# A rational layer in a four-layer convolution kernel: where the powers of its input are computed, and when

## The chip, the cores and the metric

The kernel runs on one core of a Trainium2 chip. Five engines work side by side, each through its own queue in order: TensorE (PE; PEld is its weight load), VectorE (DVE), ScalarE (ACT), GpSimd (POOL) and SyncE (SP), which only sends transfers. ACT can send transfers too. They meet at semaphores. The metric is the device time of one execution in microseconds (us); the kernel before took 11252.07 us, the median of three runs (11250.59 to 11255.03).

## The reference, cut to what matters

Four residual layers work on `x` of shape (8, 16, 128, 128) in float32. The change concerns the third, `x = x + _L2_conv_ref(_gn(x), A, Bc)`, a convolution whose weights are rational functions:

```python
def _gn(v, G=8, eps=1e-5):
    g = v.reshape(B_, G, C_ // G, H_, W_)
    ...
    return ((g - m) / jnp.sqrt(s + eps)).reshape(v.shape)

def _L2_conv_ref(x, A, Bc):          # K = 3, DEG_P = 6, DEG_Q = 4
    ...
    xp = jnp.pad(x, ((0, 0), (0, 0), (pad, pad), (pad, pad)))
    wins = jnp.stack([xp[:, :, i:i + H, j:j + W] for i in range(K) for j in range(K)])
    pw = wins[..., None] ** jnp.arange(DEG_P, dtype=x.dtype)
    P = jnp.einsum('pbchwi,fcpi->fpbchw', pw, A)
    Q = 1.0 + jnp.abs(jnp.einsum('pbchwi,fcpi->fpbchw', pw[..., 1:1 + DEG_Q], Bc))
    out = jnp.sum(P / Q, axis=(1, 3))
```

So each normalised value is needed to the powers 1 to 5; for each of the nine places of the window, each input channel and each of 16 filters there is one quotient P/Q, and the quotients are summed over places and channels.

## The kernel before

The residual `x` lies in SBUF (on-chip memory) as 128 partitions, one for each image and channel, by 128 x 128 pixels. The layers run one after the other. The rational layer has three parts.

*Powers.* `group_stats` (line 918) gives each partition its mean and `rs`, the inverse deviation. `powers(r0)`, line 929, makes the five powers of two image rows: two POOL memsets for the left and right border, the first power on DVE (L934), second and fourth as squares on ACT (L942, L944), third and fifth as products on POOL (L943, L945), each in a tile of its own with one buffer. Five transfers (L947) write them to `yd2` in DRAM, whose padded image has 130 x 130 pixels. Its top and bottom border rows are written once, from a tile of zeros (`zt`, L927).

*Turns.* `turn(r0, g)`, line 955, loads ten rows of powers of half of the images (even or odd, g) into four of the eight tiles `f`, 16 transfers on SP (L959). A row of ones in `f` stands for the power zero.

*Couples.* The work of the layer is a list of 1152 couples: 16 blocks of eight rows, two halves g of the images, two parts k of four rows, nine window places n, and two i. A block has 72 couples. For each couple PE forms the denominators `pd` and the numerators `pn` in PSUM (L971). With d the denominator, ACT takes t = |d| (two `absolute`, L992), u = ln(1 + t) (`ln`) and u = exp(-u) (`exp`, both recorded by the helper at L152), an approximate 1/(1 + t). DVE then corrects it by one Newton step: `step`, t = (1 + t)u (L1003); `times`, u = pn u (two, L1009); `ratio`, u = (t - 2)u for half of the tile (L1016). `correction` has POOL form the product v = t u of the other half (L1024). PE sums over the channels (`over_channels`, L1055), and when a group of four rows is finished DVE adds it to `x` (L1067) and takes its statistics (L1068).

The order of this loop, lines 1087 to 1119, is written by hand: the products of couple m + 1 are made beside those of couple m, and a helper `in_turn(engine, ins)` ties each ACT and DVE instruction of the couples to the one before it by an order. Within these ties a scheduler places each engine's instructions and adds the waits. The instructions of `powers` have no such tie: L1079 to L1083 call it for the first 16 rows, then the loop calls it four times in the first couple of a block, for the rows of the block after next:

```python
if (c.k, c.n, c.i) == (0, 0, 0):
    if c.g == 0 and c.r0 + 16 < H:
        for r in range(c.r0 + 16, c.r0 + 24, 2):
            powers(r)
    if c.r0 + 8 * c.g < H:
        turn(c.r0 + 8 * c.g, 1 - c.g)
c.ln()
```

Buffers: the tiles t and u have four each, v three, `pn` two, `pd` one, each power one.

Of the kernel before, what the change touches and what calls it, by code (L numbers as in the profile page):

```python
# [9 lines left out]
F32 = mybir.dt.float32  # L10
AF = mybir.ActivationFunctionType
ALU = mybir.AluOpType
# [4 lines left out]
B, C, H, W = 8, 16, 128, 128  # L17
BC = B * C
HW = H * W
HP, WP = H + 2, W + 2  # L20
# [80 lines left out]
def kernel(  # L101
# [20 lines left out]
    nc = tc.nc  # L122
# [6 lines left out]
    dram = ctx.enter_context(tc.tile_pool(name="scratch", bufs=1, space=DRAM))  # L129
# [5 lines left out]
    def k_(name):  # L135
        n, lo, hi = _WHERE[name]
        return const[:n, lo - from_ : hi - from_]
# [3 lines left out]
    sets = {AF.Exp: "exp_ln", AF.Ln: "exp_ln", AF.Tanh: "sigmoid", AF.Sigmoid: "sigmoid"}  # L141
# [36 lines left out]
    def group_stats(bn, tag):  # L178

        mv = stat.tile([BC, 2], F32, name="mv")  # L180
        nc.vector.bn_aggr(mv, bn.rearrange("p a b -> p (a b)"))
        with tc.tile_pool(name="ps_stat" + tag, bufs=1, space=PSUM) as ps:
            pm = ps.tile([BC, 1], F32, name="pm")
            mm(pm, k_("pair"), mv[:, 0:1], start=True, stop=True)
            mean = stat.tile([BC, 1], F32, name="mean")
            nc.vector.tensor_copy(mean, pm)
            dm = stat.tile([BC, 1], F32, name="dm")
            nc.vector.tensor_sub(dm, mv[:, 0:1], mean)
            e2 = stat.tile([BC, 1], F32, name="e2")
            nc.vector.scalar_tensor_tensor(e2, dm, dm, mv[:, 1:2], op0=ALU.mult, op1=ALU.add)  # L190
            pv = ps.tile([BC, 1], F32, name="pv")
            mm(pv, k_("pair"), e2, start=True, stop=True)
            var = stat.tile([BC, 1], F32, name="var")
            nc.vector.tensor_scalar_add(var, pv, EPS)

        s0 = stat.tile([BC, 1], F32, name="s0")
        lut(s0, var, AF.Sqrt)
        s1 = stat.tile([BC, 1], F32, name="s1")
        nc.vector.reciprocal(s1, s0)
        nc.vector.scalar_tensor_tensor(s1, s1, var, s0, op0=ALU.mult, op1=ALU.add)  # L200
        nc.vector.tensor_scalar_mul(s1, s1, 0.5)
        rs = stat.tile([BC, 1], F32, name="rs")
        nc.vector.reciprocal(rs, s1)
        d = stat.tile([BC, 1], F32, name="d")
        nc.vector.scalar_tensor_tensor(d, mean, -1.0, rs, op0=ALU.mult, op1=ALU.mult)
        return mean, dm, rs, d
# [3 lines left out]
    def in_turn(engine, ins):  # L210

        if engine in chain:
            tc.add_manual_dep(ins, chain[engine].name, order, reason="in turn")
        chain[engine] = ins
        return ins
# [3 lines left out]
    for n in range(5):  # L219
        t = cpool.tile([BC, BC], F32, name=f"w1_{n}")  # L220
        nc.gpsimd.memset(t, 0.0)
        for b in range(B):
            r = slice(b * C, (b + 1) * C)
# [10 lines left out]
    with ExitStack() as l0:  # L234
        wp = l0.enter_context(tc.tile_pool(name="w0", bufs=1))
        with tc.tile_pool(name="x0", bufs=2) as xp:
# [6 lines left out]
            mean0, _, rs0, d0 = group_stats(bn0, "0")  # L243
# [25 lines left out]
        for a in range(2):  # L269
            src = aff_d[:, a : a + 1].rearrange("(d p g c) a -> p g c (d a)", p=2, g=2, c=C)  # L270
            for odd in range(2):
                for g in range(2):
                    for i in range(3):
                        r = 64 * (g ^ odd) + 16 * i
# [6 lines left out]
        for i in range(3):  # L281
            for g in range(2):
                r = slice(64 * g + i * 16, 64 * g + i * 16 + 16)
# [44 lines left out]
        act = l0.enter_context(tc.tile_pool(name="act0", bufs=1))  # L328
        tmp = l0.enter_context(tc.tile_pool(name="tmp0", bufs=1))
# [326 lines left out]
        for n in range(-2, NCH + 3):  # L656
# [62 lines left out]
            if any((new, old, ahead)):  # L719
                r = var.finish()  # L720
# [42 lines left out]
    bn2 = cpool.tile([BC, NCH, 6], F32, name="bn2")  # L763
    with ExitStack() as l1:
        wp = l1.enter_context(tc.tile_pool(name="w1", bufs=1))
        tmp = l1.enter_context(tc.tile_pool(name="tmp1", bufs=3))
# [8 lines left out]
        for t, src, least in ((wa, a2, 0), (wb, q2, 1)):  # L775
            for s in range(2):
                dense = wp.tile([128, 144], F32, name="dense", bufs=2)
                nc.gpsimd.memset(dense, 0.0)
                for u in range(4):
                    for i in range(1, src.shape[0] // C + least):  # L780
                        lo, r = 32 * (u ^ s) + 4 * (i - 1), C * (i - least) + 4 * u
# [21 lines left out]
        w = wp.tile([128, 144, 9], F32, name="w")  # L803
# [11 lines left out]
        for s in range(4):  # L815
            for p in range(2):
                if 0 <= s - p < 3:
# [4 lines left out]
                    for g in range(2):  # L822
# [3 lines left out]
                            k_("image")[rows, 2 * s + g : 2 * s + g + 1],  # L826
                        )

        mean, dm, rs, _ = group_stats(bn1, "1")
        xmax = wp.tile([BC, 1], F32, name="xmax")  # L830
        nc.vector.tensor_reduce(xmax, top, AX.X, ALU.max)
# [82 lines left out]
    with ExitStack() as l2:  # L914
        wp = l2.enter_context(tc.tile_pool(name="w2", bufs=1))
        tmp = l2.enter_context(tc.tile_pool(name="tmp2", bufs=1))
        gather = k_("gather").rearrange("p (k g m) -> p k g m", k=2, g=2)
        mean, _, rs, _ = group_stats(bn2, "2")


        yd2 = dram.tile([4 * B, 20, HP, WP], F32, name="yd2")
        yv = yd2.rearrange("g (i c) h w -> g i c h w", i=5)
        zt = wp.tile([BC, WP], F32, name="zt")
        nc.gpsimd.memset(zt, 0.0)
        for i in range(5):
            for r in (0, HP - 1):
                nc.sync.dma_start(yv[:, i, :, r, :], zt)  # L927

        def powers(r0):

            y = [tmp.tile([BC, 2, WP], F32, name=f"y{i}") for i in range(1, 6)]
            nc.gpsimd.memset(y[0][:, :, 0:1], 0.0)
            nc.gpsimd.memset(y[0][:, :, WP - 1 : WP], 0.0)
            nc.vector.tensor_scalar(  # L934
                y[0][:, :, 1 : 1 + W],
                x[:, r0 * W : (r0 + 2) * W].rearrange("p (a b) -> p a b", a=2),
                mean,
                rs,
                ALU.subtract,
                ALU.mult,  # L940
            )
            nc.scalar.activation(y[1], y[0], AF.Square)  # L942
            nc.gpsimd.tensor_mul(y[2], y[1], y[0])  # L943
            nc.scalar.activation(y[3], y[1], AF.Square)  # L944
            nc.gpsimd.tensor_mul(y[4], y[3], y[0])  # L945
            for i in range(5):
                nc.sync.dma_start(yv[:, i, :, 1 + r0 : 3 + r0, :], y[i])  # L947

# [1 line left out]
        for t in fs:  # L952
            nc.gpsimd.memset(t, 1.0)

        def turn(r0, g):
            for q in range(NP):
                for u in range(4):
                    lo = 32 * (u ^ (q % 2))
                    nc.sync.dma_start(  # L959
                        fs[g * NP + q][lo : lo + 20],  # L960
                        yd2[4 * (2 * q + g) + u, :, r0 : r0 + 10, :],
                    )
# [67 lines left out]
        def products(num, ab, den):  # L1030


            todo = []
            if den:
                den.pd[1 - ab] = ps.tile([128, 2, 512], F32, name="pd")
                todo.append(product(den.pd[1 - ab], wb, *den.at(1 - ab)))
            if num:
                num.pn[ab] = ps.tile([128, 2, 512], F32, name="pn", bufs=2)
                todo.append(product(num.pn[ab], wa, *num.at(ab)))
            for _ in range(4):  # L1040
                for p in todo:
                    last["product"] = next(p)
# [33 lines left out]
            for i in range(NP // 2)  # L1076
        ]
        count = len(couples)
        for r in range(0, 10, 2):  # L1079
            powers(r)  # L1080
        turn(0, 0)
        for r in range(10, 16, 2):
            powers(r)  # L1083
        products(None, 1, couples[0])
        couples[0].absolute(0)
        products(None, 0, couples[0])
        for m in range(count + 4):
            c, before, then = (couples[i] if 0 <= i < count else None for i in (m, m - 1, m + 1))
            if c:
                c.absolute(1)  # L1090
            if c or before:
                products(before, 1, then)
            if m % 2 and m >= 3 and m - 3 < count:
                over_channels(couples[m - 3 : m - 1], 0)
            if m % 2 == 0 and m >= 4 and m - 4 < count:
                over_channels(couples[m - 4 : m - 2], 2)
            if before:
                before.times(1)
                before.ratio()
            if c:  # L1100
                if (c.k, c.n, c.i) == (0, 0, 0):
                    if c.g == 0 and c.r0 + 16 < H:
                        for r in range(c.r0 + 16, c.r0 + 24, 2):
                            powers(r)
                    if c.r0 + 8 * c.g < H:
                        turn(c.r0 + 8 * c.g, 1 - c.g)
                c.ln()
                if then:
                    then.absolute(0)
                products(c, 0, then)  # L1110
            if m % 2 and m >= 3 and m - 3 < count:
                over_channels(couples[m - 3 : m - 1], 1)
            if c:
                c.exp()
                c.step()
            if before:
                before.correction(c.stepped if c else before.stepped)
            if c:
                c.times(0)
# [6 lines left out]
    with ExitStack() as l3:  # L1126
        wp = l3.enter_context(tc.tile_pool(name="w3", bufs=1))
        tmp = l3.enter_context(tc.tile_pool(name="tmp3", bufs=2))
        mean, _, rs, d = group_stats(bn3, "3")
# [51 lines left out]
        c = curve(v, WP)  # L1181
# [284 lines left out]
```

## Time and profile before

| what | value |
|---|---|
| median of three runs | 11252.07 us |
| profiled execution | 11250.13 us, of which its span is 11248.3 us |
| granted PE clock, mean | 0.971 of full speed |
| PE busy | 8843.7 us (79%) |
| DVE busy | 9068.7 us (81%) |
| ACT busy | 8780.2 us (78%) |
| POOL busy | 4873.1 us (43%) |
| rational layer, first step to last step | 3584.05 to 10560.0 us of the span |
| POOL products for powers 3 and 5 | 64 x 1187 ns and 64 x 1140 ns |
| DVE first power | 64 x 427 ns |
| ACT squares | 64 x 417 ns and 64 x 410 ns |

The busy times of whole-span engines mix four layers with different limits, so a change in one layer is judged from that layer's stretch. In the lines below a group of instructions is named by its line, engine and operation, then out<-in by the tiles' names and shapes, the count, the busy time in us, the mean ns of one, and the idle time of the engine just before these instructions with the one that ended it.

### The profile page before, as it was taken

To read this page: it belongs to the slowest core of one execution; us is meant where nothing else is said; L and a number is where in the kernel's file an instruction comes from. 1 tells how busy PE (TensorE), PEld (TensorE's weight loads), DVE (VectorE), ACT (ScalarE), POOL (GpSimd) and SP (SyncE) were. 2 spreads that over 40 slices of the span, in tenths; PEclk is the share of its full clock that TensorE was granted. 3 is DMA by queue.
4 is the path that set the end of the run, shared out by engine and by line. 5 is a ranking of instruction groups with operands and counts; after the bars stand their busy time and mean duration, and the time that the engine had idled before them with its cause. 6 is when DMAs were issued, how large, how long until landed. Compare 5 with 4: busy or idle time off the path is not lost.

```text
span 11248.3 us, 173864 instructions
## 1 busy us (share of the span) xinstructions
PE 8843.7 (79%) x72372; PEld 2092.2 (19%) x72372; DVE 9068.7 (81%) x6829; ACT 8780.2 (78%) x7107; POOL 4873.1 (43%) x2681
## 2 busy tenths in 40 slices
PE   5999999999986777777777777777777777777788
PEld 1222222222222111111111111111111111111122
DVE  3555555555555799999999999999999999999865
ACT  2555555555545799999999999999999999999876
POOL 3555555555553633333334333334334333343300
PEclk8999999999998899999999999999999999999899
DMA  1000000000003300000000000000000000000022
GB/s 47 13 15 15 12 13 15 15 13 13 14 6 94 119 7 7 13 7 7 8 12 7 7 13 7 7 13 7 7 13 7 7 13 7 7 7 7 20 54 50
DMA packets 189391, 203.91 MB, mean 18 GB/s; under 512 B 46777, under 2 KB 155449, under 8 KB 186553
## 3 DMA queue, kind: packets, MB, share of 16 engines
q1 hardware_dynamic: 180264, 190.81, 6.4%
q8 instruction: 569, 9.32, 0.3%
q10 hardware_dynamic: 8336, 1.97, 0.1%
q14 instruction: 222, 1.81, 0.1%
HBM read 107.15 MB, written 60.04 MB: 15 GB/s over the span
## 4 chain that ended last, share of the span: by engine, by line
DVE 44%; PE 31%; ACT 14%; issue 5%; POOL 2%; DMA 1%; SPq 1%; DVEq 0%; ACTq 0%; POOLq 0%
DVE t L1003 22%; PE banks L360 17%; DVE u L1009 14%; PE pn L971 10%; ACT t L992 9%; DVE y L518 2%; PE acc L1322 2%; ACT u L152 1%; POOL y L527 1%; DVE x L538 1%; ACT hid L152 1%; PE pd L971 1%; DMA yd<-y 1%; DVE x L630 1%; SPq L1286 1%
## 5 line engine op out<-in xcount | busy, mean ns | idle before, releaser
L971 PE MATMUL pn<-f,wa 32*64 32x512 f32 x18432 | 3413.7, 625 | 1711.6 <-DVE u L1009 1687.3
L1024 POOL TENSOR_TENSOR v<-t,u 128x1024 f32<-128x1024 f32 x1152 | 2739.8, 2378 | 4017.4 <-DVE t L1003 3871.3
L1009 DVE TENSOR_TENSOR u<-pn,u 128x1024 f32<-128x1024 f32 x2304 | 2713.7, 1219 | 117.7
L971 PE MATMUL pd<-f,wb 32*64 32x512 f32 x18432 | 2601.0, 626 | 161.1 <-ACT t L992 94.6
L1003 DVE SCALAR_TENSOR_TENSOR t<-t,u 128x2048 f32<-128x2048 f32 x1152 | 2630.6, 2283 | 33.9 <-ACT u L152 33.6
L992 ACT ACTIVATE t<-pd 128x1024 f32<-128x1024 f32 x2304 | 2338.4, 1015 | 311.2 <-PE pn L971 304.7
L152 ACT ACTIVATE u<-t 128x2048 f32<-128x2048 f32 x1152 | 2202.5, 1912 | 51.9 <-PE acc L1055 15.9
L152 ACT ACTIVATE u<-u 128x2048 f32<-128x2048 f32 x1152 | 2190.7, 1902 | 0.0
L971 PEld LDWEIGHTS pn<-f,wa 32*64 32x64 f32 x18432 | 750.0, 131 | 3775.4 <-DVE u L1009 3246.1
L1016 DVE SCALAR_TENSOR_TENSOR u<-t,u 128x1024 f32<-128x1024 f32 x1152 | 1418.5, 1231 | 37.9
L152 ACT ACTIVATE hid<-banks 128x1024 f32<-128x1024 f32 x576 | 571.8, 1023 | 1049.6 <-PE banks L360 1047.7
L1055 PE MATMUL acc<-u,const 128*32 128x512 f32 x9216 | 1257.2, 618 | 1.8 <-DVE u L1016 1.8
L527 POOL TENSOR_TENSOR y<-y 128x1536 f32<-128x1536 f32 x256 | 895.0, 3496 | 833.6 <-DVE y L518 833.6
L518 DVE TENSOR_TENSOR y<-banks,vp 128x1536 f32<-128x1536 f32 x384 | 673.0, 1753 | 274.8 <-PE banks L360 271.6
L544 ACT ACTIVATE sq<-x 128x1024 f32<-128x1024 f32 x384 | 398.0, 1054 | 412.3 <-DVE x L538 289.7
L470 POOL TENSOR_TENSOR pd<-q,kp 128x1536 f32<-128x1536 f32 (+1 forms) x256 | 694.0, 2737 | 7.6 <-PE banks L360 5.9
L971 PEld LDWEIGHTS pd<-f,wb 32*64 32x64 f32 x18432 | 514.5, 132 | 751.9 <-ACT t L992 690.7
L360 PE MATMUL banks<-att,const 32*128 32x512 f32 x2304 | 499.0, 669 | 173.7 <-DVE att L509 96.0
L360 PE MATMUL banks<-h,wfc 64*128 64x512 f32 (+1 forms) x3072 | 620.5, 632 | 14.5 <-DVE h L606 14.5
L1055 PE MATMUL acc<-v,const 128*32 128x512 f32 x4608 | 616.5, 606 | 0.2 <-POOL v L1024 0.2
L606 DVE TENSOR_TENSOR h<-banks,x 128x1024 f32<-128x1024 f32 x192 | 232.6, 1211 | 437.9 <-ACT hid L152 227.6
L1322 PE MATMUL acc<-s,wspl 128*32 128x512 f32 x3072 | 389.2, 650 | 92.5 <-DVE o L1335 92.5
(181 smaller groups left out, 7329.3 us busy)
## 6 DMA issues: line engine op xcount, KB each, us to landing
f<-yd SPq DMA_DIRECT2D x512, 101.6 KB
yd<-y SPq DMA_DIRECT2D x320, 130.0 KB
xin<-in_x SPq DMA_DIRECT2D x752, 32.0 KB
four<-sil SPq DMA_DIRECT2D x256, 65.0 KB
xj<-in_x SPq DMA_DIRECT2D x8, 1024.0 KB
xl<-in_x SPq DMA_DIRECT2D x32, 256.0 KB
x1d<-xl SPq DMA_DIRECT2D x32, 256.0 KB
x<-x1d SPq DMA_DIRECT2D x8, 1024.0 KB
```

The lines of the kernel that those rows point to most:

```text
L152: ins = nc.scalar.activation(out_, in_, func, **kw).ins
L360: in_turn("pe", mm(*args, skip_group_check=True, **kw).ins)
L470: ins = nc.gpsimd.tensor_mul(t[:, :n].rearrange("p n (a b) -> p n a b", a=4), rows(self.q[d][:, k]).unsqueeze(1).to_broadcast([128, n, 4, W]),
L518: ins = nc.vector.tensor_mul(y.rearrange("p n (a b) -> p n a b", a=4), banks[:, 1:4].rearrange("p n (a b) -> p n a b", a=4), windows(v, j, 3),
L527: in_turn("pool", nc.gpsimd.tensor_add(self.y[k], self.y[k], y).ins)
L971: yield mm(p[64 * (u % 2) : 64 * (u % 2) + 64, u // 2], w[lo : lo + 32, q % 2, n].rearrange("p c f -> p (c f)"), fs[g * NP + q][lo : lo + ...
L992: in_turn("act", nc.scalar.activation(self.t[:, ab], self.pd.pop(ab), AF.Abs).ins)
L1003: ins = nc.vector.scalar_tensor_tensor(self.t, self.t, 1.0, self.u, op0=ALU.add, op1=ALU.mult).ins
L1009: ins = nc.vector.tensor_mul(self.u[:, ab], self.pn.pop(ab), self.u[:, ab]).ins
L1016: ins = nc.vector.scalar_tensor_tensor(r, self.t[:, :, 0], 2.0, r, op0=ALU.subtract, op1=ALU.mult).ins
L1024: ins = nc.gpsimd.tensor_mul(self.v, self.t[:, :, 1], self.u[:, :, 1]).ins
L1055: ins = mm(accs[k][32 * q : 32 * q + 32], gather[:, int(part == 1), g], (c.u[:, ab, 0], c.u[:, ab, 1], c.v[:, ab])[part], start=first, sto ...
```

## The change

1. `powers` becomes a generator with four steps: the first power on ACT (Identity with scale `rs` and bias `d` = -mean x rs) after the two POOL memsets; the second as a square; the fourth as a square; then the third and fifth in one DVE product (powers 2 and 4 times power 1) and the five transfers. All five powers of two rows share one tile. The steps' ACT and DVE instructions are tied into the same chains as the couples' by `in_turn`.
2. In the loop, a call starts at couples n = 0, 2, 4, 6 (i = 0, first part and half of a block), four couples apart, and takes one step per couple. It uses the tile `y`, one buffer. The step stands after `ratio` of the couple before and ahead of this couple's `ln`.
3. The first eight calls, ahead of the loop, run in groups of three, two and three, step by step together, in buffers of the tiles `t` and `u`; their second and fourth powers and half of the first turn are sent from ACT's queue.
4. `yd2` and the tile of zeros move ahead, into the layer before, with its ten transfers.

```diff
@@ -826,6 +826,15 @@
                             k_("image")[rows, 2 * s + g : 2 * s + g + 1],
                         )
 
+
+        yd2 = dram.tile([4 * B, 20, HP, WP], F32, name="yd2")
+        yv = yd2.rearrange("g (i c) h w -> g c i h w", i=5)
+        zt = wp.tile([BC, 5, WP], F32, name="zt")
+        nc.gpsimd.memset(zt, 0.0)
+        for r in (0, HP - 1):
+            for i in range(5):
+                nc.sync.dma_start(yv[:, :, i, r, :], zt[:, i])
+
         mean, dm, rs, _ = group_stats(bn1, "1")
         xmax = wp.tile([BC, 1], F32, name="xmax")
         nc.vector.tensor_reduce(xmax, top, AX.X, ALU.max)
@@ -915,36 +924,36 @@
         wp = l2.enter_context(tc.tile_pool(name="w2", bufs=1))
         tmp = l2.enter_context(tc.tile_pool(name="tmp2", bufs=1))
         gather = k_("gather").rearrange("p (k g m) -> p k g m", k=2, g=2)
-        mean, _, rs, _ = group_stats(bn2, "2")
-
-
-        yd2 = dram.tile([4 * B, 20, HP, WP], F32, name="yd2")
-        yv = yd2.rearrange("g (i c) h w -> g i c h w", i=5)
-        zt = wp.tile([BC, WP], F32, name="zt")
-        nc.gpsimd.memset(zt, 0.0)
-        for i in range(5):
-            for r in (0, HP - 1):
-                nc.sync.dma_start(yv[:, i, :, r, :], zt)
-
-        def powers(r0):
-
-            y = [tmp.tile([BC, 2, WP], F32, name=f"y{i}") for i in range(1, 6)]
-            nc.gpsimd.memset(y[0][:, :, 0:1], 0.0)
-            nc.gpsimd.memset(y[0][:, :, WP - 1 : WP], 0.0)
-            nc.vector.tensor_scalar(
-                y[0][:, :, 1 : 1 + W],
+        _, _, rs, d = group_stats(bn2, "2")
+
+        def powers(r0, name):
+
+            if name:
+                y = tmp.tile([128, 2, 2, 512], F32, name=name, bufs=4)
+                y = y.rearrange("p a b c -> p (a b c)")[:, : 10 * WP]
+            else:
+                y = tmp.tile([128, 10 * WP], F32, name="y")
+            y = y.rearrange("p (i r w) -> p i r w", i=5, r=2)
+            nc.gpsimd.memset(y[:, 0, :, 0:1], 0.0)
+            nc.gpsimd.memset(y[:, 0, :, WP - 1 : WP], 0.0)
+            ins = nc.scalar.activation(
+                y[:, 0, :, 1 : 1 + W],
                 x[:, r0 * W : (r0 + 2) * W].rearrange("p (a b) -> p a b", a=2),
-                mean,
-                rs,
-                ALU.subtract,
-                ALU.mult,
-            )
-            nc.scalar.activation(y[1], y[0], AF.Square)
-            nc.gpsimd.tensor_mul(y[2], y[1], y[0])
-            nc.scalar.activation(y[3], y[1], AF.Square)
-            nc.gpsimd.tensor_mul(y[4], y[3], y[0])
+                AF.Identity,
+                bias=d,
+                scale=rs,
+            ).ins
+            yield in_turn("act", ins)
+            yield in_turn("act", nc.scalar.activation(y[:, 1], y[:, 0], AF.Square).ins)
+            yield in_turn("act", nc.scalar.activation(y[:, 3], y[:, 1], AF.Square).ins)
+            ins = nc.vector.tensor_mul(
+                y[:, 2::2], y[:, 1::2], y[:, 0:1].to_broadcast([128, 2, 2, WP])
+            ).ins
+            in_turn("dve", ins)
             for i in range(5):
-                nc.sync.dma_start(yv[:, i, :, 1 + r0 : 3 + r0, :], y[i])
+                eng = nc.scalar if name and i % 2 else nc.sync
+                eng.dma_start(yv[:, :, i, 1 + r0 : 3 + r0, :], y[:, i])
+            yield
 
 
 
@@ -952,11 +961,11 @@
         for t in fs:
             nc.gpsimd.memset(t, 1.0)
 
-        def turn(r0, g):
+        def turn(r0, g, engines=(nc.sync,)):
             for q in range(NP):
                 for u in range(4):
                     lo = 32 * (u ^ (q % 2))
-                    nc.sync.dma_start(
+                    engines[u % len(engines)].dma_start(
                         fs[g * NP + q][lo : lo + 20],
                         yd2[4 * (2 * q + g) + u, :, r0 : r0 + 10, :],
                     )
@@ -1076,14 +1085,19 @@
             for i in range(NP // 2)
         ]
         count = len(couples)
-        for r in range(0, 10, 2):
-            powers(r)
-        turn(0, 0)
-        for r in range(10, 16, 2):
-            powers(r)
+        def together(sets):
+            for _ in range(4):
+                for c in sets:
+                    next(c)
+
+        together([powers(r, "tu"[r // 2 % 2]) for r in range(0, 6, 2)])
+        together([powers(r, "tu"[r // 2 % 2]) for r in range(6, 10, 2)])
+        turn(0, 0, (nc.sync, nc.scalar))
+        together([powers(r, "tu"[r // 2 % 2]) for r in range(10, 16, 2)])
         products(None, 1, couples[0])
         couples[0].absolute(0)
         products(None, 0, couples[0])
+        later = None
         for m in range(count + 4):
             c, before, then = (couples[i] if 0 <= i < count else None for i in (m, m - 1, m + 1))
             if c:
@@ -1097,13 +1111,16 @@
             if before:
                 before.times(1)
                 before.ratio()
+            if c and (c.g, c.k, c.i) == (0, 0, 0) and c.n % 2 == 0 and c.n < 8:
+                if c.r0 + 16 < H:
+                    later = powers(c.r0 + 16 + c.n, None)
+            if later:
+                next(later)
+                if m % 4 == 3:
+                    later = None
             if c:
-                if (c.k, c.n, c.i) == (0, 0, 0):
-                    if c.g == 0 and c.r0 + 16 < H:
-                        for r in range(c.r0 + 16, c.r0 + 24, 2):
-                            powers(r)
-                    if c.r0 + 8 * c.g < H:
-                        turn(c.r0 + 8 * c.g, 1 - c.g)
+                if (c.k, c.n, c.i) == (0, 0, 0) and c.r0 + 8 * c.g < H:
+                    turn(c.r0 + 8 * c.g, 1 - c.g)
                 c.ln()
                 if then:
                     then.absolute(0)
```

## The prediction

> **What bounds the kernel now.** I read the page first: the layers of the network follow each other, so each slice has its own limit, and in slices 15 to 37 VectorE (DVE) stands at 9 tenths. That is the rational layer. The costliest groups say what a couple, the unit of its loop, costs each engine (count, busy us, mean ns of one, idle time before):
>
> ```profile
> L1009 DVE TENSOR_TENSOR u<-pn,u 128x1024 f32<-128x1024 f32 x2304 | 2713.7, 1219 | 117.7
> L1003 DVE SCALAR_TENSOR_TENSOR t<-t,u 128x2048 f32<-128x2048 f32 x1152 | 2630.6, 2283 | 33.9 <-ACT u L152 33.6
> ...
> L1016 DVE SCALAR_TENSOR_TENSOR u<-t,u 128x1024 f32<-128x1024 f32 x1152 | 1418.5, 1231 | 37.9
> ```
>
> 1152 couples, each 2283 + 2 x 1219 + 1231 ns of DVE. Then I cut the layer in two, with the busy time of every engine (PE, PEld, DVE, ACT, POOL, then PE clock, DMA share, GB/s) and the count of L1003, one per couple:
>
> ```profile
> 3584.00:3900.00 316.00, 221.54 (x1406) 42.12 (x1403) 216.37 (x188) 221.05 (x247) 221.34 (x258) 0.76 0.38 126
> 3900.00:10560.00 6660.00, 4911.88 (x49200) 1005.10 (x49200) 6503.35 (x4537) 6309.34 (x4473) 2655.37 (x1119) 0.99 0.03 9
> ...
> 3584.00:3900.00 316.00, 75.64 (x33) 0.76 0.38 126
> 3900.00:10560.00 6660.00, 2552.66 (x1119) 0.99 0.03 9
> ```
>
> The reader should see two regimes: 33 couples in the first 316 us with no engine over 70% busy, then 1119 couples at 97.6% DVE. All 56 calls of `powers` left to the loop run in the first regime: the code puts four of them in every eighth row, but nothing ties them to a couple, and L934 runs from 3545.2 to 3890.4 and never again. The waits of that stretch (total us, times, longest) show the chain:
>
> ```profile
> DVE y L934 <- POOL y L945: 83.6, 55, 3.7
> ACT y L942 <- DVE y L934: 73.8, 38, 3.1
> ```
>
> DVE stands behind the next set's first power, which waits for POOL's fifth power of the set before (one buffer each), and POOL has its own corrections (L1024) in between. Last, a steady couple in order of time:
>
> ```profile
> 7003.48 2.28 DVE L1003 SCALAR_TENSOR_TENSOR t<-t,u 128x2048 f32<-128x2048 f32 x1
> 7003.48 1.91 ACT L152 ACTIVATE u<-t 128x2048 f32<-128x2048 f32 x1
> 7005.30 1.01 ACT L992 ACTIVATE t<-pd 128x1024 f32<-128x1024 f32 x1
> ...
> 7006.20 1.90 ACT L152 ACTIVATE u<-u 128x2048 f32<-128x2048 f32 x1
> 7008.25 1.22 DVE L1016 SCALAR_TENSOR_TENSOR u<-t,u 128x1024 f32<-128x1024 f32 x1
> 7009.40 2.28 DVE L1003 SCALAR_TENSOR_TENSOR t<-t,u 128x2048 f32<-128x2048 f32 x1
> ```
>
> The period is 5.92 us. ScalarE (ACT) runs ahead: the Ln of the next couple starts with this couple's step, and its Exp ends at 7008.10, 4.62 us after the Ln began and 1.30 us before DVE needs it. ACT alone could do a couple in 5.43 us (1.82 + 0.90 + 1.81 + 0.90 from start to start).
>
> **What the Trainium skill says.** "ScalarE: Activation LUTs", section What ACT_TABLE_LOAD costs: an ACTIVATE is 186 ns + 0.833 ns per element, each pointer operand about 93 ns more, and neighbours overlap by about 93 ns. The Silu with the same two pointers took 1442 ns for 1280 elements here; the formula gives 1438. "VectorE: DVE Perf Modes", section Why `tensor_tensor` can't do 2×_2P or 4×: two streams stay at the low rate in fp32; here the 128x512 add x<-acc,x (L1067) took 681 ns. "DMA: Bandwidth & Descriptors", section Latency and other measured facts: a transfer has a fixed cost of about 2 us; below it is 2.11 and 2.25 us. "TensorE: Matmul & The Clock Gate", Part 1: the clock halves after an idle window of about 3.4 us; here the matmul after a gap took 1.11 us where it takes 0.59.
>
> **The change, part by part.** The sum is made against the profiled execution: span 11248.3 us, 1.8 us around it, 11250.13 in all, 1.9 below the median of 11252.07.
>
> *1. The crowd at the start goes.* With the powers in the chains of ACT and DVE, built order has one call's steps in couples 0 to 3, 4 to 7, 8 to 11 and 12 to 15 of every 72, in 14 of 16 blocks. Before: the first L1003 starts at 3584.05, the 33rd at 3896.28: 32 periods in 312.2 us, where 32 x 5.92 is 189.4. Gain 122.8 us. POOL's two products vanish; it was not the bound after 3900 (40% busy), so that alone gives nothing.
>
> *2. Third and fifth power on DVE.* 2 x 260 elements: 681 x 520/512 = 0.69 us, 0.66 from start to start since neighbours overlap. It sits between L1016 and L1003 on the engine that bounds, so it counts in full: 56 x 0.66 = 37 us (34 to 40). The other 8 lie in the prologue.
>
> *3. Three short operations on ACT.* Identity 186 + 2 x 93 + 0.833 x 256 = 585 ns, an estimate from the skill's page, about 0.50 after the overlap; the squares were 417 ns (L942) and add 0.33 each. At most 0.5 in one couple, against a lead of 1.30 and a recovery of 0.49 a couple: nothing, as long as the lead is there.
>
> *4. The new wait.* The loop's calls share one tile y, one buffer. The Identity of the second, third and fourth call of a block must wait until all five transfers of the call before have landed. In the built order the SP queue sends powers 1, 2 and 4 early; the transfers of 3 and 5 follow the DVE product. That product stands just before step(3); the Identity stands on ACT between the second Abs and the Ln of couple 4, a place ACT reaches at about the same moment, since Ln of the next couple starts with the step. Behind the Identity on ACT are Ln, Abs and Exp of couple 4, and DVE's step(4) waits for that Exp. The price: issue of one transfer on SP 0.62 us from start to start, then start to landing
>
> ```profile
> 3601.18 0.69 POOL y L945
> 3601.87 0.03 issue
> 3601.89 2.11 DMA yd<-y
> ```
>
> (another 2.25), some 0.15 us of semaphores: the Identity starts 3.0 us after the product ends. Plus 0.50, plus 4.62 to the end of Exp, plus 0.05: 8.2 us. DVE's own work from the product to step(4) is 5.92 - 0.07 = 5.85. The stall is 2.3 us. While ACT stands, PE stands too (the next pd needs the Abs behind the Identity), 4.8 instead of 2.1 us; a spell of half clock then costs 0 to 0.5, since the lead is used up. I take 2.6 us (2.1 to 3.2), 3 stalls in 14 blocks: 42 x 2.6 = 109 us (88 to 134). The first call of a block finds its tile long free.
>
> *5. Prologue.* Eight calls in tiles t and u in groups instead of one buffer in a chain; two fifths of the transfers on ACT's queue, the ten border transfers moved into layer 1 (SP has time there; they were issued by 3545 and nobody waited). Before: `rs` at 3545.3, transfers f<-yd from 3567.0, first matmul 3570.3, first step 3584.05. Now: squares cannot start before POOL has cleared f and the edges, 3547.7; three groups of Identity, squares, products and ten transfers issued by ACT itself at about 0.55 us (566 for its weight transfers) give the last landing near 3561, so f goes out some 6 us earlier, but ACT still has squares and six issues to do before the first Abs. I take 4 us gained (8 gained to 3 lost). The first couples run with PE's cold clock and no lead: 4 us lost (1 to 10). In the loop SP also sends the turns' transfers; a call's five issues take some 3 us in four couples (24 us), so neither makes the other late.
>
> Sum: -122.8 + 37 + 109 - 4 + 4 = +23 us. 11250.1 + 23 is 11273; as a median of runs, 11275.
>
> **The rivals.** The balance turns on one number, the stall S: without it the sum is -86, so the break-even is S = 86/42 = 2.05 us.
>
> *A, the wait is hidden (S under 1 us; other side):* if the two late transfers landed in about 1.3 us, or ACT reached the Identity well after the product, step(4) would have its Exp in time and the change gives 86 us: 11166, at most 11208. For it: the start of the loop really is wasted, and DMA is 3% busy later, so landing may be quicker than in the crowd. Against: the two landings read are of single transfers, and ACT has no reason to be late.
>
> *B, half covered (S 1 to 2):* 11208 to 11250.
>
> *C, the stall spreads (S above 3.2, taken at 4):* cold PE delays the next Abs too and couples 5 and 6 also come late, or ACT's own DMA issues delay the first step. -86 + 168 = +82: 11334. For it: with no lead each late matmul shows; against: ACT recovers 0.49 us a couple.
>
> *D, the change does not pace the powers:* the chains hold the order in the built program, so this is excluded.
>
> **How the numbers follow.** Forecast (S 2.1 to 3.2): 0.60; A 0.10; B 0.14; C 0.16. No change is within 0.2%, 22.5 us, about what a measurement can tell here; that is S from 1.51 to 2.58. The forecast's 0.60 splits into 0.33 slower and 0.27 within, B into 0.07 faster and 0.07 within. Faster 0.10 + 0.07 = 0.17; same 0.27 + 0.07 = 0.34; slower 0.33 + 0.16 = 0.49. The range leaves out A, half of B and the far end of C: 11225 to 11315. The forecast's own range is 11254 to 11300.
>
> **What would show it.** L934's successor spread in fours over 14 blocks, and 32 periods of about 5.92 at the start: part 1. A group y<-y of 128x520 at about 0.69 us: part 2. ACT's Identity waiting for the transfer yd<-y 42 times, some 3 us each, and DVE's step waiting for ACT about 2.5 us at the same places: part 4. If the Identity waits but the step doesn't, the lead is longer than I read it, and A or B holds; if the step waits in couples 5 and 6 too, C. A first step later than 3587 makes part 5 wrong.

## The result, and the profile after

The changed kernel takes 11283.45 us (median of 9 runs, 11273.94 to 11289.23), the kernel before 11252.07 us (9 runs, 11248.15 to 11255.03): a ratio of 1.0029, with a 95% interval of 1.0018 to 1.0039. It is slower by 31 us, where 23 were forecast. The profiled execution has a span of 11286.2 us.

First the groups of the changed kernel that answer to those of before (count, then busy us, mean ns of one, idle time of the engine just before them and what ended it):

```profile
L1018 DVE TENSOR_TENSOR u<-pn,u 128x1024 f32<-128x1024 f32 x2304 | 2714.5, 1220 | 121.4 <-DVE t L1012 1.4
L1012 DVE SCALAR_TENSOR_TENSOR t<-t,u 128x2048 f32<-128x2048 f32 x1152 | 2631.9, 2285 | 122.7 <-ACT u L152 122.1
L1025 DVE SCALAR_TENSOR_TENSOR u<-t,u 128x1024 f32<-128x1024 f32 x1152 | 1414.5, 1228 | 38.1
L949 DVE TENSOR_TENSOR y<-y 128x520 f32<-128x520 f32 x56 | 38.8, 694 | 0.0
L939 ACT ACTIVATE y<-x,d,rs 128x256 f32<-128x256 f32 x56 | 33.5, 598 | 148.4 <-DMA yd<-y 136.6 <-DVE u L1018 8.7 <-DVE t L1012 3.1
```

The couple's own operations cost what they did. What is new stands in two places: the DVE step (L1012) is idle for 122.7 us ahead of itself, where it was 33.9, and what it waits for is ACT's Exp; and ACT's Identity (L939) has 148.4 us of idle time, nearly all until a transfer yd<-y. Now the layer cut in two again, with the step's line alone (us, DVE busy, count, clock, DMA):

```profile
3591.40:3791.70 200.30, 73.16 (x32) 0.95 0.06 17
3791.70:10597.00 6805.30, 2557.28 (x1120) 0.97 0.05 14
```

The first 32 periods take 200.3 us, where they took 312.2: the crowd at the start is gone. But the other couples now take 6805.3 us, or 6.08 each, where the kernel before took 5.95 on the mean after its 33rd step. The gain is paid back later, a little in each block. One place of 42, ACT, DVE and SP's queue in order of time:

```profile
7124.91 1.02 ACT L1001 ACTIVATE t<-pd 128x1024 f32<-128x1024 f32 x1 [2.20 <-PE pn L980]
7128.67 0.60 ACT L939 ACTIVATE y<-x,d,rs 128x256 f32<-128x256 f32 x1 [2.73 <-DMA yd<-y]
7129.17 1.89 ACT L152 ACTIVATE u<-t 128x2048 f32<-128x2048 f32 x1
7130.97 1.00 ACT L1001 ACTIVATE t<-pd 128x1024 f32<-128x1024 f32 x1
7131.88 1.90 ACT L152 ACTIVATE u<-u 128x2048 f32<-128x2048 f32 x1
...
7125.07 0.69 DVE L949 TENSOR_TENSOR y<-y 128x520 f32<-128x520 f32 x1
7125.68 2.29 DVE L1012 SCALAR_TENSOR_TENSOR t<-t,u 128x2048 f32<-128x2048 f32 x1
7128.07 2.35 DVE L1018 TENSOR_TENSOR u<-pn,u 128x1024 f32<-128x1024 f32 x2
7130.46 1.23 DVE L1025 SCALAR_TENSOR_TENSOR u<-t,u 128x1024 f32<-128x1024 f32 x1
7133.88 2.29 DVE L1012 SCALAR_TENSOR_TENSOR t<-t,u 128x2048 f32<-128x2048 f32 x1 [2.19 <-ACT u L152]
...
7125.79 1.16 SPq L955 DMA_DIRECT2D yd<-y  x2
```

Read it by the clock. The product of powers 3 and 5 ends at 7125.76. SP issues the two late transfers from 7125.79 to 7126.95. ACT is ready for the Identity of the next call at 7125.93, and stands for 2.73 us, until the second of them has landed and tile y is free. Then Identity, Ln, Abs, Exp in their order: the Exp ends at 7133.78, and the step that needs it starts at 7133.88. From step to step it is 8.20 us where a couple takes 5.92.

The distance from one step to the next, less 5.92, as a mean over blocks 1 to 13, places the whole of it (couple m stands for the distance from step m to step m + 1; in the kernel before nothing is over 0.06 in these couples):

| couples of the block | excess each, us | what it is |
|---|---|---|
| 2, 6, 10, 14 | 0.62 | the product on DVE |
| 3, 7, 11 | 2.47 | the stall above |
| 4, 8, 12 | 0.25 | its tail |
| 5, 9, 13 | 0.04 | nearly nothing |

### The profile page after: what moved, and what is told of

Same layout as the page of the kernel before. It is cut to its first block, busy times and chain, and to the rows that moved or that the text cites. A ratio compares the mean times of both kernels' runs of the same rounds, so it can differ in the third digit from the quotient of the medians.

```text
span 11286.2 us, 173756 instructions
## 1 busy us (share of the span) xinstructions
PE 8928.5 (79%) x72372; PEld 2115.5 (19%) x72372; DVE 9086.8 (81%) x6829; ACT 8782.5 (78%) x7171; POOL 4716.7 (42%) x2553
## 4 chain that ended last, share of the span: by engine, by line
DVE 33%; ACT 16%; PE 14%; issue 4%; DMA 1%; SPq 1%; DVEq 0%; POOL 0%; ACTq 0%; POOLq 0%
DVE t L1012 19%; DVE u L1018 12%; ACT t L1001 10%; PE pn L980 9%; ACT u L152 5%; PE acc L1339 2%; PE pd L980 2%; DMA yd<-y 1%; DVE p L1179 1%; PE far L1221 1%; PE acc L1064 0%; SPq L1303 0%; DVE s L1186 0%; DVE y L949 0%; DVE v L1171 0%
## 5 line engine op out<-in xcount | busy, mean ns | idle before, releaser
L980 PE MATMUL pn<-f,wa 32*64 32x512 f32 x18432 | 3495.2, 633 | 1636.8 <-DVE u L1018 1615.1
L980 PE MATMUL pd<-f,wb 32*64 32x512 f32 x18432 | 2636.7, 635 | 185.5 <-ACT t L1001 129.7
L1012 DVE SCALAR_TENSOR_TENSOR t<-t,u 128x2048 f32<-128x2048 f32 x1152 | 2631.9, 2285 | 122.7 <-ACT u L152 122.1
L980 PEld LDWEIGHTS pn<-f,wa 32*64 32x64 f32 x18432 | 773.3, 133 | 3694.5 <-DVE u L1018 3136.5
```

The costliest lines, as they stand in the source:

```text
L980: yield mm(p[64 * (u % 2) : 64 * (u % 2) + 64, u // 2], w[lo : lo + 32, q % 2, n].rearrange("p c f -> p (c f)"), fs[g * NP + q][lo : lo + ...
L1012: ins = nc.vector.scalar_tensor_tensor(self.t, self.t, 1.0, self.u, op0=ALU.add, op1=ALU.mult).ins
```

## The experiments

The theory was that of the forecast: tying the powers to couples removes the crowd, the product costs DVE its full time, and the one buffer of tile y costs a stall of 2.7 us at 42 places. Its rivals: the stall comes from the added work on ACT and DVE and not from the wait, or another wait stands behind it, or the crowd went because POOL lost its products. Ratios are against the kernel before, run beside it on the same chip. Three chips were used, on which its median was 11247.6 to 11251.7 us, so medians from different chips compare to within some 4 us.

### Calls of the powers eight couples apart

```diff
-            if c and (c.g, c.k, c.i) == (0, 0, 0) and c.n % 2 == 0 and c.n < 8:
+            if c and m % 72 in (0, 8, 16, 24):
                 if c.r0 + 16 < H:
-                    later = powers(c.r0 + 16 + c.n, None)
+                    later = powers(c.r0 + 16 + m % 72 // 4, None)
```

> A call of the powers starts every eighth couple (0, 8, 16, 24 of each 72) in place of every fourth; nothing else differs, tile y keeps its one buffer. Theory (the Identity's wait for the two late transfers costs 2.7 us, 42 times): the wait is gone, since four couples (24 us) lie between a call's last transfer and the next Identity; 115 us less than the changed kernel, about 11169, with no idle time of the DVE step over 0.3 us at couples 4, 12, 20. Rival (it is the three short operations on ACT and the product on DVE that cost the 2.7 us, not the wait): the stall moves with the calls and the time stays at 11275 to 11290. Rival (a wait on something else takes its place, such as the turn's transfers behind the later calls): in between, with idle time of PE before couple 36.

Measured: 11167.61 us, ratio 0.9928 (0.9915 to 0.9942), 116 us below the changed kernel's median. The step's line in this kernel, and its idle time until ACT:

```profile
L1012 DVE SCALAR_TENSOR_TENSOR t<-t,u x1152: 2274/2284/2294, 3587.3 to 10476.0; 128x2048 f32<-128x2048 f32 x192
its engine sat idle before it (us, times) until:
  ACT u L152: 15.6, 8
```

122.1 us of waiting became 15.6, of which 13.7 lie ahead of the very first step. All the work is still there (the product's 0.61 us stands in couples 2, 10, 18 and 26), so it was not the work that stalled.

### The product and the transfers one couple earlier

```diff
-            yield in_turn("act", nc.scalar.activation(y[:, 3], y[:, 1], AF.Square).ins)
+            in_turn("act", nc.scalar.activation(y[:, 3], y[:, 1], AF.Square).ins)
+            if name:
+                yield
...
             yield
+            if not name:
+                yield
```

> In the loop the product of the third and fifth power and the five transfers come one couple earlier (step 2 of a call in place of step 3); the calls stay four couples apart and share one buffer. Theory: the two late transfers now have 5.9 us more than the 2.5 to 2.8 us that they were late by, so the Identity finds its tile free: time as with calls eight couples apart, 11165 to 11180. Rival (the cost is the work, not the wait): no change, 11275 to 11290. Rival (product now waits for ACT's second square in the same couple): a new stall of up to 0.5 us at couple 2 of each call, 56 x 0.5 = 28 us of the gain lost, about 11200.

Measured: 11176.38 us, ratio 0.9936 (0.9923 to 0.9948). With the calls still four couples apart, one couple of 5.92 us between the late transfers and the next Identity is enough: the Identity of the loop's calls waits no more. The third case did not come: couples 5, 9 and 13 carry the product's 0.62 us and nothing beside it. Couple 3 of a block carries 0.46 us on the mean, in which the step waits for ACT by up to 0.81 us; it is most of the 9 us that lie between this kernel and the one above. Why ACT is late there stays open.

### All five transfers behind the product

```diff
-                eng.dma_start(yv[:, :, i, 1 + r0 : 3 + r0, :], y[:, i])
+                sent = eng.dma_start(yv[:, :, i, 1 + r0 : 3 + r0, :], y[:, i]).ins
+                if not name:
+                    tc.add_manual_dep(sent, ins.name, apart, reason="all late")
```

> All five transfers of a call in the loop wait for the DVE product (in the changed kernel three of them go out before it). Theory (wait = product's end, then the issues on SP's queue one behind the other, then the landing): three more issues of 0.6 us each in the chain, so the Identity starts 1.9 us later and each of the 42 stalls is 1.9 us longer, at about 4.4 us: 80 us more than the changed kernel, about 11363. Rival (the landing alone sets the wait, transfers and issues overlap): under 0.6 us more each, 11283 to 11308. Rival (the stall isn't this wait): no change.

Measured: 11374.09 us, ratio 1.0111 (1.0097 to 1.0125), 91 us above the changed kernel. The same place in this kernel, in order of time:

```profile
6724.69 0.69 DVE L949 TENSOR_TENSOR y<-y 128x520 f32<-128x520 f32 x1
6725.30 2.29 DVE L1014 SCALAR_TENSOR_TENSOR t<-t,u 128x2048 f32<-128x2048 f32 x1
6725.53 3.10 SPq L955 DMA_DIRECT2D yd<-y  x5
...
6730.57 0.60 ACT L939 ACTIVATE y<-x,d,rs 128x256 f32<-128x256 f32 x1 [5.62 <-DMA yd<-y]
...
6735.77 2.29 DVE L1014 SCALAR_TENSOR_TENSOR t<-t,u 128x2048 f32<-128x2048 f32 x1 [4.47 <-ACT u L152]
```

Five issues take 3.10 us on SP's queue (two took 1.16), and 1.9 us after the last of them the Identity starts, 5.19 us after the product's end where it was 2.91. The stall in couples 3, 7 and 11 is 4.6 us: it grows by 2.1 where 1.9 was expected. So the wait is a chain: product, one issue after the other, landing. The rival in which transfers overlap and only the landing counts is out.

### The third and fifth power in a tile with two buffers

```diff
-                y = tmp.tile([128, 10 * WP], F32, name="y")
+                y = tmp.tile([128, 6 * WP], F32, name="y")
+                odd = tmp.tile([128, 4 * WP], F32, name="odd", bufs=2)
```

(and the product writes odd, from which the transfers of powers 3 and 5 read). A second buffer for the whole of y, 5.2 KB a partition, was not measured.

> The changed kernel with its calls four couples apart; only the third and fifth power of the loop's calls get a tile of their own with two buffers (2.08 KB more a partition), powers 1, 2 and 4 keep one. Theory (it is the two late transfers alone that the Identity waits for; the three early ones and the product's own reads are over by then): the stall goes as it did with calls eight couples apart, 11168 (11160 to 11180), the Identity's waits for yd<-y are gone. Rival (an early transfer also ends late, behind the turn's 16 transfers on SP): the stall stays in a part of the 42 places, above 11200.

Measured: 11164.24 us, ratio 0.9923 (0.9911 to 0.9935), the lowest of all, though the 3 us to calls eight couples apart are less than two chips can tell. What the Identity waits for here:

```profile
its engine sat idle before it (us, times) until:
  DVE odd L955: 27.3, 39
  DMA yd<-u: 7.6, 2
```

The wait for yd<-y is gone. What is left is 0.7 us each, until the product has read power 1, and ACT's lead covers that: couples 3, 4, 7, 8, 11 and 12 are at 5.92 us. From the first step to the last it is 6884.64 us, 120.1 less than in the changed kernel, or 2.86 for each of 42 places. This is the same buffer rule, undone for 2 KB and for the two late transfers alone.

### Only the pacing, on the kernel before

```diff
-                    if c.g == 0 and c.r0 + 16 < H:
-                        for r in range(c.r0 + 16, c.r0 + 24, 2):
-                            powers(r)
...
+            if c and m % 72 in (0, 8, 16, 24):
+                if c.r0 + 16 < H:
+                    later = powers(c.r0 + 16 + m % 72 // 4)
+            if later and m % 4 < 3:
+                next(later)
```

(powers yields after its first power, its first square and its transfers; the first power stands in DVE's chain, the squares in ACT's.)

> The kernel before with one thing of the change alone: the loop's calls of the powers are tied to couples 0, 8, 16 and 24 of each 72, their operations in the chains of DVE (first power) and ACT (squares), a step a couple. Engines, tiles, prologue and POOL's two products stay as before. Theory (the crowd at the start was worth 122.8 us and went because the calls are tied to couples): 11250 - 123, and 56 first powers of 0.41 us (0.33 net) now inside a paced couple on DVE, + 18: about 11146. Rival (the crowd went because POOL's products left, not because of the pacing): little gain, or stalls behind POOL where its products stand between the corrections: above 11220. The 33rd step tells too: some 197 us after the first if the theory holds, 312 us if the rival does.

Measured: 11211.9 us, ratio 0.9967 (0.9954 to 0.9979), 36 us gained where 104 were expected. The 33rd step comes 194.6 us after the first, so the crowd is gone by pacing alone, as the theory has it; but 66 us of the gain are missing, and no wait shows them: DVE's step waits 2.7 us for ACT in all. The next run showed where most of them are.

### Calls eight couples apart, the products on POOL

```diff
-            ins = nc.vector.tensor_mul(
-                y[:, 2::2], y[:, 1::2], y[:, 0:1].to_broadcast([128, 2, 2, WP])
-            ).ins
-            in_turn("dve", ins)
...
+                for i in (2, 4):
+                    nc.gpsimd.tensor_mul(y[:, i], y[:, i - 1], y[:, 0])
```

(for the loop's calls; the prologue's stay on DVE.)

> As with calls eight couples apart, and the third and fifth power of the loop's calls are two products on POOL again (1.2 us each beside DVE) in place of one on DVE; the prologue keeps DVE's. Theory (the product costs DVE its 0.61 us in full, 56 times, since DVE is the bound): 34 us less than with the calls eight couples apart, 11134, which would be the fastest of all. Rival (POOL's products delay its corrections and with them the sums on PE, or slow DVE beside them): the gain is given back, 11160 or more, with idle time of PE on POOL's v in the couples with products.

Measured: 11199.02 us, ratio 0.9955 (0.9942 to 0.9969): 31 us more than with the product on DVE, where 34 less were expected. POOL and DVE in order of time, around a product on POOL (L956); L1029 is the ratio, which takes 1.22 us otherwise:

```profile
6665.84 2.38 POOL L1037 TENSOR_TENSOR v<-t,u 128x1024 f32<-128x1024 f32 x1 [3.55 <-DVE t L1016]
6666.94 1.22 DVE L1022 TENSOR_TENSOR u<-pn,u 128x1024 f32<-128x1024 f32 x1
6668.17 0.75 POOL L956 TENSOR_TENSOR y<-y 128x260 f32<-128x260 f32 x1
6668.19 1.80 DVE L1029 SCALAR_TENSOR_TENSOR u<-t,u 128x1024 f32<-128x1024 f32 x1
```

POOL's product stands right behind its correction (L1037), so it starts with the ratio, and the ratio takes 1.80 us. Nothing waits on a semaphore: the operation itself is longer by 0.58. Of the 112 products 98 stretch a ratio in this way, and the durations of all ratios show it:

```profile
L1029 DVE SCALAR_TENSOR_TENSOR u<-t,u x1152: 1212/1225/2604, 3587.5 to 10505.5; 128x1024 f32<-128x1024 f32 x192
```

(shortest, median and longest in ns.) Thirteen others begin beside the add that ends a group of rows, and there the ratio is longer by 0.1 only. From the first step to the last this kernel takes 29.3 us more than the one with the product on DVE: the ratios take 58.0 more, the product's 34.1 are saved, and the step is idle for 4.6 more. In the run before, 97 ratios are stretched, which is 56 of the missing 66 us; the other 10 I did not place. The Trainium skill names a cause ("GPSIMD Engine Reference", section Specifications): GpSimd's SBUF interfaces are shared with VectorE, and DVE instructions with two SBUF inputs contend. The trace agrees, with 1.80 us for 1.22. The ratio reads t and u from SBUF. The product with pn (L1022) has one operand in PSUM, and takes its 1.22 us beside the correction as ever.

### POOL's products beside the step

```diff
                 for i in (2, 4):
-                    nc.gpsimd.tensor_mul(y[:, i], y[:, i - 1], y[:, 0])
+                    ins = nc.gpsimd.tensor_mul(y[:, i], y[:, i - 1], y[:, 0]).ins
+                    tc.add_manual_dep(ins, chain["dve"].name, apart, reason="behind the ratio")
```

> Calls eight couples apart with POOL's two products, both now behind the ratio, so that they run beside the step (two SBUF operands, 2.28 us) in place of beside the ratio (two SBUF operands, 1.23 us, seen stretched to 1.80 with a product of 0.75 beside it). Theory (any DVE operation with two SBUF operands stands for as long as a POOL product beside it runs): the step grows by 1.2 us in 56 couples, the same loss in all as in the ratio, 11195 to 11205. Rival (only the ratio, with its strided operands, is hurt; the step is long enough to take it): the loss of 65 us goes and the time is 11134.

Measured: 11190.86 us, ratio 0.9949 (0.9935 to 0.9963), just below the theory's 11195 to 11205 and far from the rival's 11134. But the step did not grow. POOL's lines of this kernel around one call, then DVE's:

```profile
6680.07 3.41 POOL L956 TENSOR_TENSOR y<-y 128x260 f32<-128x260 f32 x2 [1.28 <-DVE u L1030]
6683.45 2.35 POOL L1038 TENSOR_TENSOR v<-t,u 128x1024 f32<-128x1024 f32 x1
```

```profile
6679.91 2.28 DVE L1017 SCALAR_TENSOR_TENSOR t<-t,u 128x2048 f32<-128x2048 f32 x1
6682.30 2.36 DVE L1023 TENSOR_TENSOR u<-pn,u 128x1024 f32<-128x1024 f32 x2
6684.69 2.20 DVE L1030 SCALAR_TENSOR_TENSOR u<-t,u 128x1024 f32<-128x1024 f32 x1
```

The step had begun 0.16 us before POOL, and it was POOL that stood: two products took 3.41 us instead of 1.5, the first of them 2.7. That pushed the correction to 6683.45, 1.1 us later than the step's end would let it start, and so into the ratio, which took 2.20 us. In all 56 calls the first product is stretched so and a ratio behind it, by 0.98 us: 55 us of ratios, where 58 were lost before. The loss came back by another door. As I had put it ("any DVE operation with two SBUF operands stands") the theory is wrong: the one that comes second stands.

### The first turn from one queue

```diff
-        turn(0, 0, (nc.sync, nc.scalar))
+        turn(0, 0)
```

> The first turn's sixteen transfers into f are all issued by SP (in the changed kernel eight of them by ACT, ahead of its last squares and the first Abs). Theory (ACT's queue is what made the first step come 1.2 us after the statistics later than before, where 4 us less was forecast): the squares start 7 us earlier, the first matmul 3 us later, and the first step comes 36 to 38 us after d is ready in place of 40.1: 2 to 4 us less than the changed kernel. Rival (the matmuls' transfers bound it): 0 to 3 us more. Either is at the edge of what the times can tell; the profile's first step is what is read.

Measured: 11293.4 us, ratio 1.0039 (1.0026 to 1.0051): no gain, rather a loss of some 10 us. The first step comes 39.7 us after d, as good as the changed kernel's 40.1, but the second comes at 51.4 in place of 46.4. ACT is free earlier (its first Abs at 28.7 us after d in place of 30.9), yet sixteen issues on SP's queue take 9.56 us and the second couple comes 5 us late. From d to the last step its profile takes 15.7 us more than that of the changed kernel; what is over these 5 lies in the loop, where nothing was changed, and stays open (the changed kernel's own nine runs are up to 15 us apart). My theory of the prologue fell: ACT's issues are not what holds the first couples up as a whole.

## Why the prediction was right, point by point

The mechanism, the sign and the two large sizes were right. The sum is closed best from the last operation of the statistics (the start of the one that makes d) to the last step, since the layers ahead are the same work: 7014.82 us before, 7044.80 after, +30.0, which fits the +31.4 of the medians.

| step of the prediction | forecast, us | measured, us |
|---|---|---|
| 1. the crowd goes | -122.8 | -122.8 (what is left over stands in the last row but one) |
| 2. product on DVE, 56 times | +37 | +34.1 (0.61 each) |
| 3. Identity and squares on ACT | 0 | 0 |
| 4. stall at tile y, 42 times | +109 (2.6 each) | +115 (2.74 each) |
| 5. prologue, d to the first step | -4 | +1.2 |
| 5. cold first couples | +4 | +0.7 |
| sum | +23 | +28 of the 30.0 |

Step 1. Nearly right. The first 32 periods took 200.3 us; taking off the four products and three stalls that now lie in them leaves 190. With the stall taken out (two buffers for the odd powers) they take 192.6, which is 189.4 and the four products and the 0.7. What I had wrong is whose gain this is: "POOL's two products vanish; ... that alone gives nothing" holds only where they stood in the crowd. Paced and left on POOL they cost some 57 us of DVE's time, so pacing alone is worth 36, and the gain of 122.8 needs both parts of the change. A sign of it was in the trace of before, behind the mean of 1187 ns for L943 (shortest, median and longest in ns):

```profile
L943 POOL TENSOR_TENSOR y<-y,y x64: 721/734/2535, 3548.2 to 3893.0; 128x260 f32<-128x260 f32 x64
```

Of these products 46 took 0.72 to 0.74 us, and 15 took 2.53, all behind a DVE step that had begun shortly before.

Step 2. Right; the duration of 0.69 us was exact, and 0.61 from start to start where I took 0.66. The price is paid in full, since DVE is the bound. Even so it is the cheaper place: one product of 0.61 on DVE stands against two ratios stretched by 0.58.

Step 3. Right. The Identity took 598 ns (585 estimated) and the squares 415 and 420; with calls eight couples apart no stall shows in their couples.

Step 4. Right in its terms. The Identity stood at all 42 places (39 put down to yd<-y, 136.6 us, or 3.5 each; three to DVE). It started 2.91 us after the product's end at the place shown, 3.08 on the mean of the 42 and 2.85 to 4.47 in all (3.0 forecast). From the product's end to the delayed step it is 8.12 us there (8.2 forecast), which leaves a stall of 2.28 (2.3 forecast). The mean of the 42 is 2.46, and 0.25 follows in the next couple. That tail goes with PE's clock, for which the forecast had set 0 to 0.5: it is 0.26 to 0.37 us at the 32 places where at least 1.9 of the last 3 us ahead of the delayed step ran at half the clock, and at most 0.07 at the ten where at most 1.6 did. The three experiments that took the wait away without the work gained 107 to 119 us, and the one that made it longer lost 91. The stall lay in the forecast's span (2.1 to 3.2) and above the break-even of 2.05 that I had named: 42 x (2.74 - 2.05) is 29 us, the whole of the result. Rivals A and B (the landing is quick, or ACT is late) fell with the 3.08; C fell too, since couples 5 and 6 come on time.

Step 5. Wrong in sign, and small. The transfers f<-yd did start earlier (17.1 us after d where it was 21.8 before), but the first Abs came at 30.9 after d, where it was 30.0. In that profile ACT issued eight of the turn's transfers in 6.97 us, and its last squares started behind them; moving them to SP helped the first Abs and not the couples. In the other profiles with the same prologue the first step came 40.2 to 43.6 us after d, and the old prologue gave 38.9 and 43.3. I can say that the 4 us are not there; what the prologue is worth within some 4 us stays open. The first couples lost 0.7 us where 4 were forecast. That the two errors of this step nearly cancel, +5.2 and -3.3, is luck.

One thing that isn't the change: in this profile d itself came 6.2 us later than in that of before. Over ten profiles it lay between 3538.3 and 3551.4 us, with the code ahead of it old (3538.3, 3545.2) or new (3539.9 to 3551.4), so a difference of this size between two profiles is scatter, and the sum has to be made from d on.

## What to carry to other kernels

When a change shares one buffer between calls that follow each other, time the chain from the last producer to the release (product, issue after issue, landing: 2.9 us here) against the lead of the engine that waits; a lead short by less than half a couple, 42 times, cost 115 us, and 2 KB for the late parts alone, or the producer one couple earlier, gave nearly all of it back. A break-even worked out for the one uncertain number tells what to measure first. Before work goes to GpSimd because it looks idle, see which DVE operations it would run beside, and whether they have an operand in PSUM. Read the shortest and the longest of a group beside its mean.

## What the runs showed of the hardware that I had not expected

In these runs a POOL product of two SBUF tensors and a DVE operation of two SBUF tensors do not run beside each other, and whichever begins second is stretched: the ratio from 1.22 to 1.80 us behind a product of 0.75 us that had begun 0.02 us earlier, and POOL's product from 0.73 to 2.71 us behind a step that had begun 0.16 us earlier. The second one takes most of its own time after the end of the first: over the kernel before and the three with products on POOL, a ratio (1.22 us alone) that began during a product ended 1.08 us after it every time, and a product (0.73 alone) that began during a step or a ratio ended 0.59 to 0.61 us after that one. No wait is shown for it; it is seen only in the durations of single instructions. The mean of a group hides it: with the products on POOL 1152 ratios have a mean of 1276 ns and a median of 1225, with a longest of 2604, where with the product on DVE the longest is 1406. The DVE product with one operand in PSUM was untouched beside 2.37 us of POOL: its longest is 1.227 us in all ten profiles.
